# A two-layer MetaFormer kernel: 48 rows of image 0's convolution on VectorE, and the end of the third front dealt out among the first expert blocks

## The chip, the cores and the metric

The kernel runs on one NeuronCore of one Trainium2 chip. A time is the device time of one execution in microseconds (us). The kernel before took 3087.72 us, the median of three runs (3082.57 to 3088.3). The engines are named as in the profile: PE is TensorE (PEld its weight loads), DVE is VectorE, ACT is ScalarE, POOL is GpSimd, SP is SyncE, which here only issues transfers.

## The reference

Four images of 384 channels by 32x32 pixels (1024 tokens each) go through two layers:

```python
# layer 0
x = x + attention_with_relative_tables(ln_c(x))            # 8 heads
t = to_tokens(x); t = t + gelu(ln_t(t) @ kron(fc1, fc2).T) @ kron(proj1, proj2).T
# layer 1
x = x + dwconv7x7 + dwconv5x3 + dwconv3x5 + two separable pairs + bias   (of ln_c(x))
t = to_tokens(x); t = t + sum over 2 of 4 experts of gate * (gelu(ln_t(t) @ w1 + b1) @ w2 + b2)
x = from_tokens(t)
```

All depthwise kernels of layer 1 are folded into one 7x7 kernel per channel: 49 taps, each a multiply and an add over an image. The gate picks two of four experts for each token, so the rows of the expert stage are only known once an image has gone through its convolution.

## The kernel before, in words

Three stages follow each other. The projection to q, k, v and the attention take the first 1500 us and are not touched. `rest_phase` does everything after the attention, and the change lies in it.

For each image b the work of `rest_phase` is a row of generators; each `yield` is a step, and carries two costs, one for DVE and one for PE, in estimated us.

- `front(b)` (called by `enter`): loads, `project` (attention output projection, L977 and L980, then token statistics, L87 to L97) for two halves of 512 tokens, then `net` for each half. `net` is the small feed-forward net: `u_ps` (L999), DVE's `u` (L1001), twelve `f_ps` (L1012, a 32-row matmul), twelve Gelus on ACT (L1022), twelve `o_ps` (L1016), ACT's copy `o`, three `ffn_ps` (L1029) and three DVE additions into `xb` (L1030). The `f_ps` tiles rotate over the PSUM banks in `banks`: three banks of tag "h", and for image 0 three more from the pool `ps_y`.
- `normalise` (with front in `ahead`): per half the token statistics (`row_ps`, L87; `s_st`, L89; `s_rstd`, L96), two `all_ps` (L117, from `s_dg`, L115), and DVE's `xc` (L1061). `image` writes the padded image `img` (L1068).
- `convolve(b)`: for each of 49 taps DVE runs one multiply-add (L1089) for each of three chunks of 128 channels, over 32 rows. Its instructions keep the order in which they are issued. For image 0 (`first`) DVE only has chunk 0 and the first `own` rows of chunk 1; `taps_by_matmul` does the rest on PE with diagonal matrices (L1137, L1148) and adds it with L1151.
- `dispatch(b)`: `gates` (gate logits `gate_ps`, L661; statistics; softmax; top two), `scatter` (`before_ps`, L755; slot positions, ending with `pos`, L778; the list of expert blocks, `block_list`, ending with `slot`, L872; and 16 indirect transfers on POOL, L1205, that write the image's rows to `xs_d`).
- `blocks(g)`: the expert blocks of group g, 13, 16, 16 and 22 of them, 67 in all. A block is 128 rows: a gather `xg` by POOL (L1250), three transposes `xT_ps` (L1263), twelve times three `e_ps` (L1301), a Gelu (L1304) and a `y_ps` (L1279), then DVE's `yo` (L1282) and a store. POOL fetches weights `w` (L1269) into four tiles; a tile is free only after the `yo` of an earlier block. The first gather of group g waits for the rows that all dispatches up to image g have written (`g["after"]`).

What sets the order: each engine runs its instructions in one order. Image 0's `first` is dealt by hand with `ahead(1)`, then `dispatch(0)` with `ahead(2)`. Afterwards the loop in `more` deals the generator `todo` (`others()`: convolution 1, dispatch 1, convolution 2 together with front 3, dispatch 2, convolution 3, dispatch 3) among the expert blocks: after each `y` step it adds 0.05 to DVE's clock and 1.36 to PE's, and takes steps of `todo` as long as DVE's clock is behind PE's. When a group's blocks are all issued and the next group's rows are not, the rest of that dispatch is issued at once.

A position in the expert stage is counted below in blocks: 9.58 means that 9 blocks and 7 of 12 `y` steps of the tenth stand ahead on PE.

Of the kernel before, what the change touches and what calls it, by code (L numbers as in the profile page):

```python
# [19 lines left out]
B, C, IMG = 4, 384, 32  # L20
# [80 lines left out]
def result(steps):  # L101

    while True:
        try:
            next(steps)
        except StopIteration as end:
            return end.value


def to_partitions(nc, pools, ident, one, values):  # L110

    small, psum, tag = pools
    nj = values.shape[1]
    dg = small.tile([P, nj, P], F32, tag="s_dg", name="s_dg", bufs=1)
    nc.vector.tensor_tensor(dg, bcast(ident.unsqueeze(1), 1, nj), bcast(values, 2, P), ALU.mult)  # L115
    ps = psum.tile([P, TOK], F32, tag=tag, name="all_ps")
    nc.tensor.matmul(ps, one, dg.rearrange("p j n -> p (j n)"), start=True, stop=True)  # L117
    return ps


def center(nc, psum, tag, one, w):

    n = w.shape[2]
    for c in range(0, n, C):
        part = w[:, :, c : min(c + C, n)]
        ps = psum.tile([P, part.shape[2]], F32, tag=tag, name="sum_ps")
        for k in range(KC):
            nc.tensor.matmul(ps, one, part[:, k, :], start=(k == 0), stop=(k == KC - 1))
        for k in range(KC):
            nc.vector.scalar_tensor_tensor(part[:, k, :], ps, -1.0 / C, part[:, k, :], ALU.mult, ALU.add)  # L130
# [763 lines left out]
def rest_phase(tc, cst, x, ao_d, ins, xs_d, y_d, x2_d, out):  # L894
# [9 lines left out]
    with ExitStack() as es:  # L904
# [7 lines left out]
        ps_h = es.enter_context(tc.tile_pool(name="r_ps_h", bufs=3, space=PSUM))  # L912
        ps_y = es.enter_context(tc.tile_pool(name="r_ps_y", bufs=1, space=PSUM))
# [73 lines left out]

        def net(b, xs, rstd):

            banks = [(ps_h, "h", None)] * 3 + ([(ps_y, "y", 2)] * 2 + [(ps_y, "t", None)] if b == 0 else [])  # L990
            if True:
                scale = to_partitions(nc, (small, ps_m, "m"), ident, one, rstd)
                scale_sb = work.tile([P, TOK], F32, tag="scale", name="scale")
                nc.scalar.copy(scale_sb, scale)


                ps = ps_m.tile([P, TOK], F32, tag="m", name="u_ps")
                for k in range(KC):
                    nc.tensor.matmul(ps, fold[:, k, :], xs[:, k, :], start=(k == 0), stop=(k == KC - 1))  # L999
                u = small.tile([P, TOK], F32, tag="u", name="u")  # L1000
                nc.vector.tensor_tensor(u, ps, scale_sb, ALU.mult)  # L1001
                yield 1.4, 3.5

                po = ps_m.tile([P, TOK], F32, tag="m", name="o32_ps")
                pend = []
                for f0 in range(0, NF + 3, 3):
                    phs = []
                    for f in range(f0, min(f0 + 3, NF)):
                        pool, tag, bufs = banks[f % len(banks)]
                        ph = pool.tile([P, TOK], F32, tag=tag, name="f_ps", **({"bufs": bufs} if bufs else {}))  # L1010
                        lo = f % 4 * 32
                        nc.tensor.matmul(ph, c1t[lo : lo + 32, f // 4, :], u[lo : lo + 32, :], start=True, stop=True)  # L1012
                        phs.append((f, ph))
                    for f, hs in pend:
                        lo = f % 4 * 32
                        nc.tensor.matmul(  # L1016
                            po[lo : lo + 32, :], cp1t[:, f, :], hs, start=(f < 4), stop=(f >= NF - 4)
                        )
                    pend = []
                    for f, ph in phs:  # L1020
                        hs = hid.tile([P, TOK], F32, tag="hs", name="hs", bufs=HS)
                        nc.scalar.activation(hs, ph, AF.Gelu)  # L1022
                        pend.append((f, hs))
                    yield 0.0, 2.2
                o32 = small.tile([P, TOK], F32, tag="u", name="o32")
                nc.scalar.copy(o32, po)
                for m in range(KC):
                    ps = ps_h.tile([P, TOK], F32, tag="h", name="ffn_ps")
                    nc.tensor.matmul(ps, spread[:, m * P : (m + 1) * P], o32, start=True, stop=True)  # L1029
                    nc.vector.scalar_tensor_tensor(  # L1030
                        xs[:, m, :], ps, cp2[:, m : m + 1], xs[:, m, :], ALU.mult, ALU.add
                    )
                yield 2.1, 2.7
# [31 lines left out]
        def image(halves):  # L1065
            rows = IMG // 2
            for half, (xc, scale_sb) in enumerate(halves):
                nc.vector.tensor_tensor(  # L1068
                    img[:, :, 3 + half * rows : 3 + (half + 1) * rows, 3 : 3 + IMG],
                    xc.rearrange("p k (y x) -> p k y x", x=IMG),  # L1070
                    bcast(scale_sb.rearrange("p (y x) -> p y x", x=IMG).unsqueeze(1), 1, KC),
                    ALU.mult,
                )
                yield 1.7, 0.0
# [30 lines left out]
        def preload(w, keep=lambda ins_: ins_, which=range(2)):  # L1105
            for fh in which:
                keep(nc.sync.dma_start(w[fh], ins["w12"][fh * P : (fh + 1) * P, :]))
# [272 lines left out]
        def dispatch(b, pause=0.0):  # L1380
            yield from gates(b)
            yield from scatter(b, pause)

        def ahead(b, halves):
            if b < B:
                yield from enter(b)
                yield from normalise(xbs[b], halves)

        def first(halves, later):


            half, own = IMG // 2, 20
            taps = taps_by_matmul(xbs[0], made, [(2, 0, half), (2, half, half), (1, own, IMG - own)])
            yield from image(halves)
            for i, _ in enumerate(convolve(0, xbs[0], [(0, 0, IMG), (1, 0, own)])):
                for _ in range(1 + i % 4 // 2 + (i % 5 == 0)):
                    next(taps, None)
                if i % 7 < 5:
                    next(later, None)
                if i == 48:  # L1400
                    for steps in (taps, later):
                        for _ in steps:
                            pass
                yield
            preload(wts[1])

        def others():

            later = iter(())
            for b in range(1, B):
                if b > 2:
                    yield from image(halves[b])
                side, later = later, ahead(b + 1, halves[b + 1]) if b > 1 else iter(())
                for t, cost in enumerate(convolve(b, xbs[b], [(k, 0, IMG) for k in range(KC)])):
                    for start, steps in ((2, side), (12, later)):
                        more = next(steps, None) if t >= start else None
                        if more:  # L1420
                            cost = cost[0] + more[0], cost[1] + more[1]
                    yield cost
                yield from side
                yield from later
                later = dispatch(b, 0.0 if b == 2 else 2.6)
                if b == 1:
                    yield next(later)
                    yield from image(halves[2])
                    yield from later
            yield 6.0, 0.0  # L1430
            yield from later
# [9 lines left out]
        rstd0 = result(project(xs0, at0))  # L1441
        rstd1 = result(project(xs1, at1))
        result(net(0, xs0, rstd0))
        side = normalise(xbs[0], halves[0], (0,))
        for _ in net(0, xs1, rstd1):
            next(side, None)
# [3 lines left out]
        for _ in combined:  # L1450
            pass
        center(nc, ps_m, "m", one, gw)
        todo = others()
        made = diagonals((2, 1))
        for _ in first(halves[0], ahead(1, halves[1])):
            pass
        later = ahead(2, halves[2])
        for i, _ in enumerate(dispatch(0)):
            if i == 0:
                result(image(halves[1]))  # L1460
            for j in range(3 if i > 5 else 0):
                next(later, None)
                if i > 10 and (i + j) % 2:
                    next(todo)
        result(later)
        clock = [0.0, -8.0]

        def spend(steps):
            cost = next(steps, None)
# [125 lines left out]
```

## Time and profile before

| what | us |
|---|---|
| median of three runs | 3087.72 |
| time of the profiled execution | 3092.57 |
| its span | 3090.6 |
| PE busy | 2929.9 (95%) |
| DVE busy | 1956.6 (63%) |
| image 0's convolution, about | 1590 to 1737 |
| dispatch 0 and front 2, about | 1737 to 1842 |
| expert blocks with convolutions 1 to 3 | 1842 to 2560 |
| expert blocks alone, results | 2560 to 3090 |

The spans are from the start of the profiled execution. Where a line of the trace gives several numbers, they are the start, the duration, the engine, the line of the kernel and the operation, then the count, and in brackets the idle time of the engine before it and what ended that.

### The profile page before, as it was taken

The page shows a single profiled execution, that of the slowest core. Times are in us where ns is not written, and L with a number is a line of the kernel's source. Part 1 is how long each engine was busy: PE and PEld are TensorE (multiplying, and loading weights), DVE is VectorE, ACT ScalarE, POOL GpSimd, SP SyncE. Part 2 cuts the span into 40 slices and gives each one's busy share as a digit, 9 for nine tenths or more (in the row PEclk, how much of TensorE's full clock was granted, in tenths as well). Part 3 has the DMA queues.
Part 4 walks back from the last instruction along what each step waited for, and adds up shares of the span by engine and source line. Part 5 has one row for each costly group of instructions (what it writes and reads, how often), then busy time and mean ns, then how long its engine had stood idle before and what let it go on. Part 6 is the DMA issues. An engine that isn't in the chain of part 4 may idle for free.

```text
span 3090.6 us, 63376 instructions
## 1 busy us (share of the span) xinstructions
PE 2929.9 (95%) x25391; PEld 2020.6 (65%) x25391; DVE 1956.6 (63%) x3575; ACT 1370.8 (44%) x2833; POOL 1170.7 (38%) x1132
## 2 busy tenths in 40 slices
PE   8997999999999999999899789999999989999996
PEld 4544676777677677776533347776577867777775
DVE  2226787878787877777568869999899640001101
ACT  1104666666767666666322232333342243233332
POOL 3223747473747473737400122252124231124412
PEclk9998999999999999999999879999999999999998
DMA  3796565656565656564500314734243065366742
GB/s 123 259 320 212 130 203 131 206 132 203 134 202 134 200 131 196 136 199 128 186 21 34 128 31 156 274 136 154 75 175 132 26 229 215 134 227 250 263 180 72
DMA packets 262791, 500.55 MB, mean 162 GB/s; under 512 B 134736, under 2 KB 186832, under 8 KB 254816
## 3 DMA queue, kind: packets, MB, share of 16 engines
q1 hardware_dynamic: 169168, 247.12, 26.0%
q0 software_dynamic: 43424, 227.84, 20.0%
q10 hardware_dynamic: 49904, 21.53, 3.6%
q8 instruction: 200, 3.28, 0.5%
q14 instruction: 95, 0.78, 0.1%
HBM read 543.58 MB, written 152.37 MB: 225 GB/s over the span
## 4 chain that ended last, share of the span: by engine, by line
PE 67%; DVE 13%; issue 11%; POOL 4%; DMA 3%; ACT 2%; another core or an unknown queue 0%; SPq 0%; POOLq 0%; DVEq 0%; ACTq 0%
PE e_ps L1301 12%; PE y_ps L1279 12%; DVE xb L1089 8%; PE t_ps L410 7%; PE av_ps L227 7%; PE sc_ps L227 7%; PE tabq_ps L227 5%; PE a_ps L420 3%; PE tv_ps L227 2%; PE proj_ps L977 2%; PE tabk_ps L227 1%; PE tap_ps L1137 1%; DVE extra L402 1%; PE f_ps L1012 1%; PE o_ps L1016 1%
## 5 line engine op out<-in xcount | busy, mean ns | idle before, releaser
L1301 PEld LDWEIGHTS e_ps<-xT,w 128*128 128x128 f32 x4824 | 656.5, 193 | 217.7 <-issue 14.6
L353 POOL TENSOR_TENSOR bias<-b,s 128x416 f32<-128x416 f32 (+24 forms) x656 | 659.2, 1042 | 178.1 <-DMA s<-sd 157.5
L1301 PE MATMUL e_ps<-xT,w 128*128 128x128 f32 x4824 | 670.6, 277 | 14.1 <-DVE xb L1030 5.0
L1279 PE MATMUL y_ps<-w,eh 128*128 128x384 f32 x1608 | 651.9, 490 | 17.2 <-ACT eh L1304 14.8
L1089 DVE SCALAR_TENSOR_TENSOR xb<-img,pack,xb 128x1024 f32<-128x1024 f32 (+1 forms) x539 | 634.7, 1241 | 0.0
L1304 ACT ACTIVATE eh<-e_ps,w 128x128 f32<-128x128 f32 x804 | 292.9, 367 | 725.3 <-PE e_ps L1301 669.5
L1269 POOL DMA_INDIRECT w<-in_w,row x134 | 171.4, 1279 | 749.7 <-PE y_ps L1279 301.4
L402 DVE TENSOR_REDUCE extra<-arow 128x32 f32<-128x32 f32 (+24 forms) x768 | 381.3, 555 | 9.4 <-ACT arow L391 5.7
L381 DVE CUSTOM_DVE_ANT_0 arow<-sc_ps,bias 128x1024 f32<-128x1024 f32 x256 | 312.5, 1221 | 107.1 <-issue 55.5
L410 PEld LDWEIGHTS t_ps<-ident,arow 128*128 128x128 f32 x2048 | 221.2, 142 | 175.9 <-ACT aT L411 100.6
L391 ACT ACTIVATE arow<-arow,nm 128x1024 f32<-128x1024 f32 x256 | 302.4, 1181 | 70.8 <-DVE nm L381 70.8
L411 ACT COPY aT<-t_ps 128x512 f32<-128x512 f32 x512 | 278.6, 603 | 95.3 <-PE t_ps L410 95.0
L410 PE MATMUL t_ps<-ident,arow 128*128 128x128 f32 x2048 | 283.2, 282 | 17.1 <-ACT arow L391 17.0
L1282 DVE TENSOR_TENSOR yo<-y_ps,w 128x384 f32<-128x384 f32 x67 | 37.0, 553 | 396.0 <-PE y_ps L1279 387.8
L227 PE MATMUL sc_ps<-kk,qs 48*32 48x512 f32 x4096 | 279.2, 608 | 7.7 <-DVE nm L381 6.7
L1279 PEld LDWEIGHTS y_ps<-w,eh 128*128 128x128 f32 x1608 | 248.3, 193 | 31.9 <-ACT eh L1304 19.4
L227 PEld LDWEIGHTS av_ps<-aT,vb 128*64 128x64 f32 x4096 | 222.3, 137 | 52.0 <-ACT aT L411 40.4
L227 PE MATMUL av_ps<-aT,vb 128*64 128x128 f32 x4096 | 237.7, 274 | 0.0
L318 DVE STREAM_TRANSPOSE b<-tabk_ps 128x480 f32<-128x480 f32 x256 | 218.4, 983 | 23.5 <-PE tabk_ps L227 22.2
L227 PE MATMUL tabk_ps<-tab,kq 48*128 48x480 f32 x512 | 223.0, 582 | 6.1 <-DVE b L318 6.1
L227 PE MATMUL tabq_ps<-tab,kq 48*128 48x480 f32 x512 | 220.1, 579 | 2.1 <-ACT aT L411 1.4
L322 ACT COPY st<-tabq_ps 128x480 f32<-128x480 f32 x256 | 142.3, 560 | 71.0 <-PE tabk_ps L227 45.0
(211 smaller groups left out, 3163.4 us busy)
## 6 DMA issues: line engine op xcount, KB each, us to landing
sd<-st SPq DMA_DIRECT2D x128, 480.0 KB
s<-sd SPq DMA_DIRECT2D x256, 240.0 KB
xs_d<-zero POOLq DMA_DIRECT2D x8, 3072.0 KB
tvw<-in_tv SPq DMA_DIRECT2D x120, 192.0 KB
y_d<-yo SPq DMA_DIRECT2D x67, 192.0 KB
qk_d<-qk_sb POOLq DMA_DIRECT2D x48, 256.0 KB
qs<-qk_d SPq DMA_DIRECT2D x256, 48.0 KB
kq<-qk_d ACTq DMA_DIRECT2D x56, 192.0 KB
```

The source lines that it names most:

```text
L227: ins = nc.tensor.matmul(*args, **kw)
L318: turn = nc.vector.transpose(b2.rearrange("p e y x -> p x (e y)")[:, i + j], ps[:, j, : SPAN * IMG])
L353: nc.gpsimd.tensor_tensor(bias[:, y0:y1, :], bass.AP(b2.tensor, b2.offset + (e * IMG + y0) * IMG, [list(b2.ap[0]), [(step * IMG + 1) * IMG ...
L381: nc.vector.tensor_tensor_reduce(s["flat"], ps.rearrange("p h n -> p (h n)"), s["bias"].rearrange("p y x -> p (y x)"), -SCALE, BIG, ALU.ad ...
L391: nc.scalar.activation(s["flat"], s["flat"], AF.Exp, bias=s["nm"], scale=-1.0, accum_out=dn[:, y % YT : y % YT + 1])
L402: pin(nc.vector.tensor_reduce(ex[:, i, :], a[:, p0:p1, :].rearrange("p y x -> p x y"), AX.X, ALU.add))
L410: pin(nc.tensor.transpose(pt[:, j, :], s["flat"][:, k0 : k0 + P], ident))
L411: pin(nc.scalar.copy(aT[:, 4 * g : 4 * g + 4, s["y"] % YB, :], pt))
L1089: ins_ = nc.vector.scalar_tensor_tensor(acc[:, k, y0:y1], img[:, k, dy + y0 : dy + y1, dx : dx + IMG], w7[:, k, dy, dx : dx + 1], acc[:, k ...
L1279: nc.tensor.matmul(py, hs, w[:, o : o + C], start=(ff == 0), stop=(ff == NF - 1))
L1301: nc.tensor.matmul(ph, w[:, o : o + P], xT[k][:, c, :], start=(c == 0), stop=(c == KC - 1))
L1304: nc.scalar.activation(hs, ph, AF.Gelu, bias=w[:, o : o + 1])
```

## The change

Four edits. Image 0: DVE takes 16 rows of chunk 1 instead of 20 (48 rows with chunk 0), PE the other 16, and the taps are dealt at a slightly different pace. `net` of image 2 also uses the three banks of `ps_y`. During `dispatch(0)` two steps of front 2 are taken per step instead of three, and one step of convolution 1 instead of one or two alternately; what is left of front 2 is not finished on the spot, but goes step by step with `todo`. The clock of DVE's work starts at -15 instead of -8.

```diff
 def net(b, xs, rstd):
-    banks = [(ps_h, "h", None)] * 3 + ([(ps_y, "y", 2)] * 2 + [(ps_y, "t", None)] if b == 0 else [])
+    banks = [(ps_h, "h", None)] * 3 + ([(ps_y, "y", 2)] * 2 + [(ps_y, "t", None)] if b in (0, 2) else [])
...
 def first(halves, later):
-    half, own = IMG // 2, 20
+    half, own = IMG // 2, 16
...
-        for _ in range(1 + i % 4 // 2 + (i % 5 == 0)):
+        for _ in range(1 + i % 4 // 2 + (i % 4 == 0)):
             next(taps, None)
...
+def mixed(some, others_):
+
+    while True:
+        steps = [next(s, None) for s in (some, others_)]
+        if not any(steps):
+            return
+        yield tuple(sum(c) for c in zip(*filter(None, steps)))
...
 for i, _ in enumerate(dispatch(0)):
     if i == 0:
         result(image(halves[1]))
-    for j in range(3 if i > 5 else 0):
+    for _ in range(2 if i > 5 else 0):
         next(later, None)
-        if i > 10 and (i + j) % 2:
-            next(todo)
-result(later)
-clock = [0.0, -8.0]
+    if i > 10:
+        next(todo)
+todo = mixed(later, todo)
+clock = [0.0, -15.0]
```

## The prediction

> **What bounds the kernel now.** First the page's slices (40 of 77 us each). The change touches slices 21 to 31.
>
> ```profile
> PE   8997999999999999999899789999999989999996
> ...
> DVE  2226787878787877777568869999899640001101
> ...
> PEclk9998999999999999999999879999999999999998
> ```
>
> PE is above 90% nearly everywhere; the hole is the front stage (slices 22 to 24), where its clock drops too. DVE is as full as PE in the five slices after it. Next, windows over these stretches (busy time of each engine, granted clock, DMA):
>
> ```profile
> core 0: us, PE busy (x) PEld busy (x) DVE busy (x) ACT busy (x) POOL busy (x), PEclk, DMA share, GB/s
> 1780.00:1790.00 10.00, 10.00 (x30) 2.18 (x26) 0.14 (x3) 3.37 (x6) 7.09 (x8) 0.59 0.33 111
> ...
> 1820.00:1830.00 10.00, 5.89 (x29) 3.46 (x28) 9.60 (x23) 0.30 (x1) 1.00 (x1) 0.79 0.08 25
> ...
> 1840.00:1990.00 150.00, 149.40 (x912) 118.37 (x911) 149.80 (x170) 44.47 (x120) 37.76 (x24) 1.00 0.46 174
> 1990.00:2058.00 68.00, 65.20 (x393) 49.13 (x392) 61.44 (x156) 31.37 (x69) 38.03 (x27) 1.00 0.65 247
> 2058.00:2390.00 332.00, 323.42 (x1848) 231.87 (x1846) 321.04 (x484) 118.99 (x274) 82.94 (x62) 0.99 0.34 126
> ```
>
> From 1840 to 2390 both engines are full: no slack on either. Third, the timeline of PE: image 0's net (six banks, first two lines) and image 2's (three banks).
>
> ```profile
> 1543.69 1.99 PE L1012 MATMUL f_ps<-u,pack 32*128 32x512 f32 x12 [1.08 <-DVE u L1001]
> 1545.61 1.92 PE L1016 MATMUL o_ps<-hs,pack 128*32 128x512 f32 x6
> ...
> 1773.46 2.97 PE L1012 MATMUL f_ps<-u,pack 32*128 32x512 f32 x6 [1.19 <-ACT hs L1022]
> 1776.36 1.93 PE L1016 MATMUL o_ps<-hs,pack 128*32 128x512 f32 x6
> ```
>
> A float32 matmul is two instructions here, so the x12 are six f and the x6 three. Image 2's take twice as long after the wait of 1.19 us for a bank. DVE meanwhile stands 12.44 us before L1030. Last, and decisive, the start of a group: image 1's gate on PE and group 1's first transposes; POOL's first and last row writes, weights and gather; then the chain at group 2's start.
>
> ```profile
> 1993.36 2.77 PE L661 MATMUL gate_ps<-xb,pack 128*32 128x512 f32 x12
> ...
> 2057.79 0.49 PE L1263 MATMUL xT_ps<-ident,xg 128*128 128x128 f32 x3
> ```
> ```profile
> 2018.45 1.01 POOL L1205 DMA_INDIRECT xs_d<-rows,pos  x1 [5.29 <-DVE b_prod L860]
> ...
> 2048.25 0.96 POOL L1205 DMA_INDIRECT xs_d<-rows,pos  x1 [0.30 <-issue]
> 2049.51 2.10 POOL L1269 DMA_INDIRECT w<-in_w,row  x1 [0.30 <-issue]
> 2051.92 2.07 POOL L1250 DMA_INDIRECT xg<-xs_d,slot  x1 [0.31 <-issue]
> ```
> ```profile
> 2386.52 2.48 DVE xb L1089 x2
> ...
> 2389.03 3.48 DMA xg<-xs_d,slot
> ...
> 2392.64 0.89 PE xT_ps L1263 x3
> ...
> 2394.08 4.21 PE e_ps L1301 x18
> ```
>
> Group 1's rows land just as PE gets there; at group 2 PE already waits some 4 us for the gather. From gate to next group there is a latency that PE has to cover with blocks of the old group, and it has nothing to spare.
>
> **What the Trainium skill says.** "TensorE: Matmul & The Clock Gate", Part 1, has PE at half clock after an idle window of about 3.4 us: the trace agrees in the factor (1.14 us for six f instructions at 1771, 2.97 at 1773). The same page, under "Architectural detail", calls VectorE a strict FIFO: agrees, ready L1089 instructions stand behind L1030 for 12.44 us. "SBUF — State Buffer", "Who interferes with whom", has GpSimd blocked by VectorE instructions with two SBUF inputs: compatible with row writes of 0.97 or 2.0 us while L1089 runs. "ScalarE: Activation LUTs", "What ACT_TABLE_LOAD costs", gives about 1283 ns; the trace has 1283.
>
> **Part by part.** Positions are read from the built kernels' order on each engine.
>
> *48 rows.* A DVE step of 1024 and 640 elements takes 2.01 us (ten instructions in 10.04), three of 1024 take 3.6: so 0.81 for 640, 1.0 ns an element, 49 x 0.13 = 6.4 us less. PE's 196 tap instructions grow from 64x384 to 64x512: 0.082 to 0.112 us apiece (20 less 8 instructions: 1.35 us; 48 less 8 at 384: 3.3), 5.9 us more. From 1620 to 1690 PE is the fuller one (DVE idles 14 us), and the last tap sum now has two steps behind it, not one. I take 0, between -4 (DVE alone decides) and +3.
>
> *Six banks for image 2.* No instruction more. A half at full clock takes 9.7 us (1543.7 to 1553.4), against 18.3 (1771.1 to 1789.4). If the clock still drops, the first six f at 1.99 and the rest at half rate (six f at 2.87 / 3, twelve o at 1.93 / 3): 15.5. DVE now has one step of convolution 1 (3.7 us) ahead of `u`, so f starts about 3 us later, at 1774.4, after more PE idle time than in image 0's case (3 us against 1.1). So half clock is likely in at least one half; I take one of two.
>
> *The rest of front 2 in the blocks.* The first e_ps comes at 1774.4 + 15.5 + 9.6 (half to half, as before: 1789.4 to 1799.0) + 9.7 + 1.3 (xT) = 1810.5, against 1830. The moved part (one ffn, 12 + 12 transposes, four all_ps, four table loads) costs PE in the blocks what front 3 costs there: the two yo intervals around it (2211.9, 2235.6, 2254.8) are 10.7 us above two blocks of 16.1, and 2.6 for ffn. It issues no transfer; on SP image 1's store and image 3's loads fall behind eleven stores of y instead of nine, but front 3 reads them only at 16.9, some 90 us on. Counted as if all blocks ran evenly from it, the start is 1810.5 + 13.3 = 1823.8; before it is 1993.4 - 9.58 x 16.1 = 1839.1. Gain 15.3 (9.5 both halves at half clock, 21 none).
>
> *Convolution 1 and dispatch 1 come later in the order.* Four steps fewer before the blocks, the clock at -15, and front 2's costs put image 1's gate at position 11.25 instead of 9.58, behind yo 10 instead of yo 8. DVE needs 14.9 us for its twelve taps and yo, PE 16.1 a block, so DVE waits at every yo and cannot be early: the gate runs at 1823.8 + 11.25 x 16.1 = 2004.9, 11.5 later than before. From gate to the first block then: 25.1 to the first write (1993.36 to 2018.45), 26 for sixteen writes (27.5 before without the two weight fetches, 24.6 at group 2), 7.8 from the last write's end to e_ps (2386.3 to 2394.1): 58.9 us. PE has 1.75 blocks and 9.3 us of gate work for it: 37.5. It waits 21 us for the gather, where it waited for nothing, and starts cold (half clock for 6.8 us, 3.4 lost). All sixteen writes now stand on POOL behind group 0's last fetch and ahead of group 1's first, so that fetch waits too, but it is no later than the gather. Group 1 starts 11.5 + 58.9 + 3.4 - 64.4 = 9.5 us later than before.
>
> *Group 2.* Image 2's gate moves from 22.75 to 23.5, its before_ps from 26.33 to 27.08: `rank` (L759) follows yo 26 by one tap instead of yo 25 by four, 16.1 - 3.8 = 12 us later against group 1's start. The 46 us from L759 to group 2 (2347.8 to 2394.1) are the same. Shift 9.5 + 12 = 21.5. A second count on DVE alone: between the two slot lists both kernels have 231 taps, but yo 13 now makes DVE idle about 14 us: 22. After group 2 nothing waits (image 3's gate is at 35.17 in both, group 3 at 45) and the shift reaches the end.
>
> **Sum.** On the profiled execution: 3090.6 + 0 + 21.5 = 3112 span, 2 more for its time. The median of the runs is 4.9 below the profiled time: 3087.7 + 21 = 3109.
>
> **Rivals.** *Faster:* the saved front is kept, because gate to first block takes less than PE's cover. It decides below 37.5 us at the first gate; the rows' writes would have to go in about 5 us. Then 15 to 21 us are gained: 3070. For it: PE's hole is real. Against: sixteen writes never took less than 21.7 us (image 0's). *Only the first gate waits:* DVE catches up in the wait and image 2's dispatch is not late: +9.5, 3097. Against: DVE's order ties it to yo 26. *Cancels:* full clock in both halves and 22 us of writes at the first gate, no second wait: 3087. *DVE loses more,* both halves at half clock and DVE's waits at front 3 on top: +33, 3121.
>
> **Chances.** Both waits, 3098 to 3117: 0.68. First gate only: 0.12. Worse: 0.07. Cancels: 0.04. Faster: 0.09. Change that this measurement can't tell from none is 0.2%, 6 us. Slower 0.86, the same 0.05, faster 0.09. The range 3088 to 3123 leaves out the faster case and little above.
>
> **What would show it.** f_ps of image 2 in runs of twelve instructions; first e_ps near 1810; gate of image 1 near 2005; POOL's sixteen writes unbroken, ending near 2056; PE idle about 20 us before group 1's first xT_ps and 10 to 15 before group 2's, DMA xg as releaser. No such idle time at group 1, or a gate before 1990, makes me wrong.

## The result and the profile after

The changed kernel took 3119.3 us (median of 3106.17, 3119.91, 3125.24 and 3118.7), the kernel before 3087.94 on the same chip (four runs each): 1.0101 times as long, with an interval of 1.0077 to 1.0124. That is 31 us slower, where 21 were forecast. In profiled executions the difference is smaller, 3106.17 against 3092.57 us (spans 3104.2 and 3090.6): the profiled execution after is the fastest of its four, and the one before is longer than its median. So the changed kernel was profiled a second time, on another chip (e4_again, 3116.3 us of span), and this execution is near its median. Below, these two are the first and the second profile after.

The slices of the page of the kernel after, the same rows as before:

```profile
PE   8997999999999999999899899979998999999996
...
DVE  2226787878787878787477879879999740001101
...
PEclk9998999999999999999999899989999999999998
```

The hole in the front (slices 23 and 24: 78 before) is nearly filled, 89, and the clock with it (87 before, 89 after). Two new holes stand further on: a 7 in slice 27, with an 8 of clock, and an 8 in slice 31. Windows over the same stretches of the kernel after, with one more for the second hole:

```profile
1780.00:1790.00 10.00, 10.00 (x35) 3.44 (x32) 7.53 (x15) 3.34 (x6) 7.40 (x7) 1.00 0.29 98
1820.00:1830.00 10.00, 9.86 (x52) 6.63 (x51) 7.97 (x14) 1.58 (x4) 0.88 (x1) 1.00 0.05 20
1840.00:1990.00 150.00, 149.49 (x914) 118.47 (x914) 140.99 (x167) 47.55 (x122) 39.02 (x26) 1.00 0.60 226
1990.00:2058.00 68.00, 47.47 (x268) 34.75 (x267) 55.51 (x149) 25.16 (x52) 24.98 (x18) 0.86 0.36 126
...
2390.00:2420.00 30.00, 10.72 (x53) 8.30 (x52) 29.45 (x34) 2.77 (x8) 23.54 (x15) 0.66 0.26 86
```

From 1820 to 1830 PE is busy for 9.86 us instead of 5.89. Between 1990 and 2058 it is busy for 47.5 instead of 65.2, and from 2390 on for 10.7 of 30. And DVE, which had no slack from 1840 to 1990 (149.8 of 150), now idles 9 us there: its convolution steps were dealt out later. From the first e_ps to image 1's gate it idles 28 us (before 2.9), most of it in one wait before L1030.

What opened the holes is in the timelines of the kernel after. PE: image 1's gate and the first transposes of group 1. POOL: first and last row write, weights, gather. Then the chain of work (the steps that ended last) at group 2's start.

```profile
2000.09 2.77 PE L661 MATMUL gate_ps<-xb,pack 128*32 128x512 f32 x12
...
2061.62 0.90 PE L1263 MATMUL xT_ps<-ident,xg 128*128 128x128 f32 x3 [20.08 <-DMA xg<-xs_d,slot]
```
```profile
2029.11 1.03 POOL L1205 DMA_INDIRECT xs_d<-rows,pos  x1 [30.23 <-DVE b_change L853]
...
2053.80 2.02 POOL L1205 DMA_INDIRECT xs_d<-rows,pos  x1 [0.31 <-issue]
2056.13 1.04 POOL L1269 DMA_INDIRECT w<-in_w,row  x1 [0.30 <-issue]
2058.23 1.25 POOL L1250 DMA_INDIRECT xg<-xs_d,slot  x1 [1.06 <-DMA xs_d<-rows,pos]
```
```profile
2404.87 3.69 DVE xb L1089 x3
...
2408.57 4.19 DMA xg<-xs_d,slot
...
2412.90 0.89 PE xT_ps L1263 x3
...
2414.34 3.81 PE e_ps L1301 x18
```

The 16 writes are unbroken, and PE waits 20.08 us for the gather behind them; before, the first transposes of group 1 had no wait. At group 2 PE waits 18.7 us (before 4.0).

A table of five points is the ruler for everything below, because image 0's gate alone varies by 7 us between the profiles of this study. All are us from that gate (`gate_ps`, 1736.68 before, 1733.45 and 1737.74 after); in brackets PE's wait for xg.

| profile | first e_ps | image 1's gate | group 1's first xT_ps | group 2's first xT_ps | end of span |
|---|---|---|---|---|---|
| before | 93.7 | 256.7 | 321.1 (0) | 656.0 (4.0) | 1353.9 |
| after | 72.4 | 266.6 | 328.2 (20.1) | 679.5 (18.7) | 1370.8 |
| after, once more | 79.8 | 274.0 | 335.5 (22.4) | 685.8 (18.7) | 1378.6 |

The first e_ps comes 14 to 21 us earlier; at image 1's gate this has turned into a loss of 10 to 17, at group 2 of 24 to 30.

### The profile page after: what moved, and what is told of

It reads as the page before. It is cut to its first block, busy times and chain, and to the rows that moved or that the text cites. A ratio compares the mean times of both kernels' runs of the same rounds, so it can differ in the third digit from the quotient of the medians.

```text
span 3104.2 us, 63372 instructions
## 1 busy us (share of the span) xinstructions
PE 2921.3 (94%) x25391; PEld 2014.4 (65%) x25391; DVE 1950.2 (63%) x3575; ACT 1375.0 (44%) x2835; POOL 1179.6 (38%) x1132
## 4 chain that ended last, share of the span: by engine, by line
PE 74%; DVE 9%; issue 8%; DMA 4%; POOL 3%; ACT 2%; SPq 0%; another core or an unknown queue 0%; POOLq 0%; ACTq 0%; DVEq 0%
PE e_ps L1301 16%; PE y_ps L1279 15%; PE t_ps L410 7%; PE sc_ps L227 7%; PE av_ps L227 7%; PE tabq_ps L227 5%; DVE xb L1089 4%; PE a_ps L420 3%; PE tv_ps L227 2%; PE tap_ps L1137 1%; PE proj_ps L977 1%; POOL bias L353 1%; PE tabk_ps L227 1%; DMA s<-sd 1%; PE f_ps L1012 1%
## 5 line engine op out<-in xcount | busy, mean ns | idle before, releaser
L1301 PE MATMUL e_ps<-xT,w 128*128 128x128 f32 x4824 | 671.3, 277 | 13.6 <-ACT xT L1264 6.5
L1089 DVE SCALAR_TENSOR_TENSOR xb<-img,pack,xb 128x1024 f32<-128x1024 f32 (+1 forms) x539 | 628.4, 1229 | 0.0
L1279 PEld LDWEIGHTS y_ps<-w,eh 128*128 128x128 f32 x1608 | 247.5, 193 | 28.3 <-ACT eh L1304 15.4
L1205 POOL DMA_INDIRECT xs_d<-rows,pos x64 | 80.7, 1260 | 295.8 <-DVE b_prod L860 231.3
```

Source lines behind the costliest of these rows:

```text
L1089: ins_ = nc.vector.scalar_tensor_tensor(acc[:, k, y0:y1], img[:, k, dy + y0 : dy + y1, dx : dx + IMG], w7[:, k, dy, dx : dx + 1], acc[:, k ...
L1279: nc.tensor.matmul(py, hs, w[:, o : o + C], start=(ff == 0), stop=(ff == NF - 1))
L1301: nc.tensor.matmul(ph, w[:, o : o + P], xT[k][:, c, :], start=(c == 0), stop=(c == KC - 1))
```

## The experiments

The runs were made in three sets of four, each set on another chip, with the kernel before beside them (3082.8, 3080.2 and 3068.6 us): so the ratios are compared, and times from different sets are not. Ratios are to the kernel before on the same chip, with their intervals; where a ratio is put in us, it is its difference from 1 (or from another ratio) times 3085 us. Of e2_rows, e5_early, e8_half, e10_early_nobanks and e11_earlier the profiled execution is 4 to 9 us faster than the median of the runs, so their points belong to a fast execution, as those of the first profile after do.

**e1_banks: only the banks.** The kernel before with

```diff
-    ... if b == 0 else [])
+    ... if b in (0, 2) else [])
```

> The kernel before with one edit: image 2's net uses six PSUM banks. My account: the order of the instructions is the same as before on every engine (image 1's gate at position 9.58), so nothing else becomes late; the two halves of the net shorten from 18.3 us each to between 9.7 and 15.5, the first e_ps moves from 1830 to between 1812 and 1820, DVE's wait before L1030 (21.4 us) shrinks by as much, and the whole expert stage moves with it: 10 to 18 us faster, about 3074, with xT_ps of group 1 at about 2043 and no wait there. Rival, DVE is the bound of this stretch and the banks only move the wait: within 5 us of the kernel before. Rival, PE's half clock in the net has nothing to do with the banks: the halves stay at 18 us, no change.

Measured: 0.9975 (0.9966 to 0.9984), 8 us faster; first e_ps at 89.0, image 1's gate at 252.4, group 1 at 316.5, group 2 at 650.6. The sign is as expected, the size below the range of 10 to 18 us. Timeline of PE in this run, the two halves of image 2's net:

```profile
1764.97 1.99 PE L1012 MATMUL f_ps<-u,pack 32*128 32x512 f32 x12 [0.85 <-DVE u L1001]
...
1790.72 2.97 PE L1012 MATMUL f_ps<-u,pack 32*128 32x512 f32 x12 [2.58 <-DVE u L1001]
1793.62 1.99 PE L1016 MATMUL o_ps<-hs,pack 128*32 128x512 f32 x6
1795.54 2.08 PE L1012 MATMUL f_ps<-u,pack 32*128 32x512 f32 x6
```

The first half starts at full clock (twelve instructions in 1.99) and takes 14.4 us, 2.4 of them idle; the second, after an idle time of 2.58, falls to half clock and takes 14.9. Before it was 18.2 and 17.8. All that is gained at the first e_ps (4.7 us) is still there at group 2 (5.4): with the order of the work unchanged, a saved front is kept.

**e2_rows: only the rows.** The kernel before with

```diff
-            half, own = IMG // 2, 20
+            half, own = IMG // 2, 16
...
-                for _ in range(1 + i % 4 // 2 + (i % 5 == 0)):
+                for _ in range(1 + i % 4 // 2 + (i % 4 == 0)):
```

> The kernel before with one edit: VectorE has 16 rows of chunk 1 of image 0 instead of 20 and the pace of the taps goes with it. The prediction took 0 (between -4 and +3); the profile of the changed kernel had image 0's gate at 1733.45 instead of 1736.68, so 3 us faster: 3085. Rival: PE is the bound and the gate is not earlier: 3088 to 3091.

Measured: 1.0003 (0.9993 to 1.0012), no difference; the prediction's 0 was right, and the 3 us that I read out of the first profile after were not the edit's. The rival has the mechanism. On this chip image 0's gate stood at 1730.27 with 16 rows and at 1730.19 with 20 (e1_banks). Only the wait before it is shorter (4.14 us against 7.54): PE, with more taps, is later, and DVE still ends the wait. DVE's saving went into longer waits for PE: from 1590 to 1731 us it stands 13.7 us before L1030 (9.7 with 20 rows) and 4.0 before `u` (2.2).

**e3_deal: only the dealing.** The changed kernel with 20 rows, the old pace and three banks for image 2, so `mixed`, the steps of `dispatch(0)` and the clock at -15 are what is left of the change.

> The changed kernel without its other two edits: 20 rows and three banks in image 2's net as before, but front 2 and convolution 1 dealt as in the changed kernel. My account: the dealing is the whole loss and more, image 1's gate stays at position 11.25 and PE waits about 20 us at group 1 and about 19 at group 2, while the banks' gain is missing: 15 to 20 us slower than the changed kernel, about 3136. Rival, the banks are worth nothing here: the same as the changed kernel, 3119. Rival, the loss comes from the banks or the rows: 3088.

Measured: 1.0175 (1.0158 to 1.0192), 54 us slower than the kernel before; the changed kernel in the same set 1.0103. So the dealing, with its clock at -15, is the whole loss, and the other edits take 22 us of it back, where 15 to 20 were expected. That is more than e1_banks, for a reason that the timeline of PE shows:

```profile
1778.12 1.13 PE L1012 MATMUL f_ps<-u,pack 32*128 32x512 f32 x6 [0.85 <-DVE u L1001]
1794.16 0.90 PE L1263 MATMUL xT_ps<-ident,xg 128*128 128x128 f32 x3 [14.91 <-DMA xg<-xs_d,slot]
1794.99 2.08 PE L1012 MATMUL f_ps<-u,pack 32*128 32x512 f32 x6
```

Here the first transposes of group 0 stand in PE's order between two groups of f, where their rows are not yet there, and the whole net waits 14.91 us behind them. In the changed kernel they stand behind both halves. The edits are not independent: banks and rows also decide where this instruction falls.

**e4_again: the changed kernel once more.**

> The changed kernel once more. Its first four times were 3106.2 to 3125.2 us, and the mean granted clock of the three long ones was 0.972 against 0.976: 0.004 of 3110 us is 12 us of full clock, or 25 us more at half clock. My account: the net of image 2 runs at full clock in some executions and at half in others; a profile near 3120 shows x12 f_ps of 3 us and more in both halves and a first e_ps near 1815 to 1820. Rival: the two waits of PE vary (writes of rows, 25 to 30 us): then e_ps is at 1806 again and the waits at groups 1 and 2 are 5 to 10 us longer together.

Measured: 1.0103 (1.0086 to 1.012), and a profile of 3116.3 us. Timeline of PE, first half of image 2's net, in the first profile after (upper) and in this one (lower):

```profile
1770.83 3.40 PE L1012 MATMUL f_ps<-u,pack 32*128 32x512 f32 x12 [0.57 <-DVE u L1001]
...
1775.97 1.12 PE L1012 MATMUL f_ps<-u,pack 32*128 32x512 f32 x2
...
1780.05 1.13 PE L1012 MATMUL f_ps<-u,pack 32*128 32x512 f32 x6
```
```profile
1774.86 4.37 PE L1012 MATMUL f_ps<-u,pack 32*128 32x512 f32 x12 [0.57 <-DVE u L1001]
...
1781.01 2.07 PE L1012 MATMUL f_ps<-u,pack 32*128 32x512 f32 x2
...
1788.73 2.08 PE L1012 MATMUL f_ps<-u,pack 32*128 32x512 f32 x6
```

The same instructions, with the same waits before them (2.05 and 0.57 us): in one execution the clock is back some 5 us after the first f, in the other only for the last 2 of the half's 19.3 us. The two halves take 13.0 and 12.1 us there, 19.3 and 13.5 here. That is 7.7 us more; the first e_ps is 7.4 later from image 0's gate, and the end 7.8 (1378.6 and 1370.8). The rival, longer waits, has 2.3 us at group 1 and nothing at group 2. The rest of the 12 us between the spans had passed before image 0's gate, which is 4.3 us later here.

**e5_early: the same kernel, gates earlier.** The changed kernel with

```diff
-        clock = [0.0, -15.0]
+        clock = [0.0, 8.0]
```

> The changed kernel with one number: DVE's clock starts at 8 instead of -15. More of convolution 1 is issued before the blocks, and image 1's gate stands at position 9.75 again (11.25), image 2's before_ps at 26.5 (27.08), nearly as in the kernel before. My account (the positions make the waits): from gate to group 1's first xT_ps about 62 us passed in every run so far; DVE had 10.5 us of idle time left between 1830 and 1990, so the gate can come about 10 us earlier, the wait at group 1 goes, and from group 1 to group 2 it is 335 us again instead of 351: 24 us less than the changed kernel, about 3094. Rival, the new dealing of front 2 loses the time, wherever the gate stands: 3112 to 3120. Rival, DVE falls behind and PE waits for yo: also above 3110, with PE idle before y_ps in the first blocks.

Measured: 0.9993 (0.9984 to 1.0002); the ratio of the changed kernel is 1.0101, so one number is worth 33 us. Nothing of front 2, the banks or the rows is touched. Timeline of PE in this run:

```profile
1980.67 2.77 PE L661 MATMUL gate_ps<-xb,pack 128*32 128x512 f32 x12
...
2043.57 0.52 PE L1263 MATMUL xT_ps<-ident,xg 128*128 128x128 f32 x3 [1.18 <-DMA xg<-xs_d,slot]
```

From gate to group it is 62.9 us, much as in the changed kernel (61.5); but the gate is 22 us earlier, at 244.6, and the wait is 1.18. Group 2 starts at 645.8 after a wait of 7.5. The direction was expected and the size was not (24): I had counted DVE's idle time from 1830 on only. DVE also stood 20.7 us before L1030 in the changed kernel, and with more convolution steps ahead of it 6.6 here. In this profile group 2 starts 10 us earlier than before (645.8 and 656.0), but by the ratio the runs gain only 2.

**e6_late: the kernel before, gates later.**

```diff
-        clock = [0.0, -8.0]
+        clock = [0.0, -25.0]
```

> The kernel before with one number: DVE's clock starts at -25 instead of -8. Nothing of front 2 and no bank is changed, only image 1's gate goes to position 10.67 (9.58) and image 2's before_ps to 27.0 (26.33). My account: the gate comes about 17 us later (1.09 blocks of 16.1), group 1's first xT_ps waits some 12 us for the gather and is about 15 us later, group 2's waits 12 to 16: 25 to 30 us slower than the kernel before, about 3111. Rival, the loss of the changed kernel comes from front 2's rest between the blocks and not from the order of the gates: within 6 us of the kernel before.

Measured: 1.009 (1.0073 to 1.0107), 28 us slower. This is what was expected. First e_ps at 95.1, near its place before (93.7); image 1's gate at 274.4, group 1 at 330.9 after a wait of 9.7, group 2 at 678.8 after 15.1. Timeline of PE in this run, image 1's gate and the first transposes of groups 1 and 2:

```profile
2005.43 2.77 PE L661 MATMUL gate_ps<-xb,pack 128*32 128x512 f32 x12
...
2061.85 0.87 PE L1263 MATMUL xT_ps<-ident,xg 128*128 128x128 f32 x3 [9.66 <-DMA xg<-xs_d,slot]
...
2409.75 0.87 PE L1263 MATMUL xT_ps<-ident,xg 128*128 128x128 f32 x3 [15.05 <-DMA xg<-xs_d,slot]
```

So a loss nearly as large as the changed kernel's comes without any of its other edits, by the place of the gates alone.

**e7_both: banks, rows and the gates a little earlier.** The kernel before with both edits and `clock = [0.0, 0.0]`.

> The kernel before with the six banks for image 2, the 16 rows, and DVE's clock at 0 instead of -8: image 1's gate at position 9.08, image 2's before_ps at 25.83. My account: the banks' 7.7 us stay, DVE is full before image 1's gate, so group 1 is not earlier, but image 2's dispatch is 8 us ahead and the wait of 4 us at group 2 and the half clock after it go: 3070 to 3073. Rival, DVE's extra six instructions ahead of the first yo make PE wait for yo: 3077 or more.

Measured: 0.9995 (0.9985 to 1.0005), no gain, against the expectation. Image 1's gate is at 241.2 and image 2's `before_ps` 12 us earlier than before, but PE still waits 4.04 us at group 2. POOL's timeline of this run:

```profile
2350.33 1.94 POOL L1205 DMA_INDIRECT xs_d<-rows,pos  x1 [0.30 <-issue]
2354.59 1.95 POOL L1269 DMA_INDIRECT w<-in_w,row  x1 [2.32 <-DVE pause L1097]
2356.84 2.01 POOL L1205 DMA_INDIRECT xs_d<-rows,pos  x1 [0.31 <-issue]
...
2380.03 0.97 POOL L1205 DMA_INDIRECT xs_d<-rows,pos  x1 [0.30 <-issue]
```

A fetch of weights stands between the second and the third write and waits for a tile, and eight of the sixteen writes take the long time of about 2 us (before: four): 32.9 us from the first write to the end of the last (2348.06 to 2381.00), 24.6 before. An earlier `pos` only helps if POOL's queue lets it. The rival has its part too: up to 2050 PE waits 2.3 us for `yo` and 4.7 for weights, whose tile a `yo` has to free.

**e8_half and e9_half1: half of the writes.** The changed kernel without half of the row writes, so that half of the rows are missing in the expert stage, for images 1 and 2 (e8_half) or image 1 alone (e9_half1; there the condition is `b == 1`),

```diff
-                for s in range(2):
+                for s in range(0 if b in (1, 2) and j > 3 else 2):
                     write(rows, im["pos"][:, j, s : s + 1])
```

> The changed kernel with half of the 16 row writes of images 1 and 2 left out, so that half of these images' rows are missing in the expert stage. Positions of gates as in the changed kernel. My account: the writes are a link of the chain from the gate to the next group; eight of them take 13 us less (1.63 us each), so PE's waits for xg shrink from 20 and 19 us to about 7 and 6, if the gates themselves keep their times, and the kernel takes about 26 us less than the changed one: 3092. Rival, the block list on DVE or the weights' fetch ends the wait, not the writes: waits as before, 3117.

> The changed kernel with half of the 16 row writes of image 1 alone left out (half of that image's rows are missing in the expert stage); image 2 writes all. Positions as in the changed kernel. The question is whether the first wait counts, or only the second. My account: both waits add up; group 1 starts about 13 us earlier, image 2's gate with it, the wait at group 2 stays at 19 us: about 15 us less than the changed kernel, 3102. Rival, the wait at group 1 is given back at group 2: group 2 starts when it did and its wait grows to 30 us: 3117.

Measured: e8_half 1.0004 (0.9992 to 1.0015), e9_half1 1.0065 (1.005 to 1.0079). In us below the changed kernel: 30 and 11. PE in e8_half, starts of groups 1 and 2:

```profile
2046.13 0.90 PE L1263 MATMUL xT_ps<-ident,xg 128*128 128x128 f32 x3 [8.02 <-DMA xg<-xs_d,slot]
...
2383.46 0.52 PE L1263 MATMUL xT_ps<-ident,xg 128*128 128x128 f32 x3 [0.88 <-DMA xg<-xs_d,slot]
```

From gate to group 1 it is 47.3 us in e8_half and 47.2 in e9_half1 instead of 61.5: eight writes are 14 us, and the writes, not the block list, are the last link. In e9_half1 group 1 comes at 317.4, its wait is 8.0; group 2's wait is 16.3 and the way between them 353.7 (351.3): the waits add up, and about 2 of the 14 us are given back.

**e10_early_nobanks: what the banks are worth once the gates are in time.** e5_early with three banks for image 2.

> The kernel e5_early (changed kernel with DVE's clock at 8) with three banks for image 2's net. Image 1's gate stands at position 9.75, before_ps of image 2 at 26.5. My account: with the gates in time, the banks are worth what they were worth in the kernel before, 8 us (the two halves of the net 18 us each instead of 12 to 17): about 3086. Rival, the banks are worth 20 us in the new dealing, as the difference of e3_deal and the changed kernel: about 3098.

Measured: 1.0027 (1.0016 to 1.0038); e5_early has 0.9993, so the banks are worth 10 us. Group 1 stands at 317.4 and group 2 at 657.9, 10 and 12 later than in e5_early. The 8 us of the first account are nearer than the rival's 20.

**e11_earlier and e12_fill: a faster version.** e11_earlier is the changed kernel with `clock = [0.0, 16.0]`. e12_fill is the kernel before with six banks, the rows, and

```diff
-                if i > 10 and (i + j) % 2:
+                if i > 10 and (i + j) % 3:
                     next(todo)
...
-        clock = [0.0, -8.0]
+        clock = [0.0, -15.0]
```

> The changed kernel with DVE's clock at 16: image 1's gate at 9.25, image 2's before_ps at 26.0. My account: DVE is full before image 1's gate, so group 1 is not earlier than in e5_early, but the 7.5 us wait at group 2 shrinks to 0 to 4: 3070 to 3075, the fastest of this study. Rival, six more taps ahead of the first yo hold PE up in the first blocks: 3080 or more.

> The kernel before with the six banks, the 16 rows, and during dispatch 0 convolution 1's steps taken at two of three steps of front 2 instead of one of two, with DVE's clock at -15 to make up for it (image 1's gate at position 9.0, image 2's before_ps at 25.75). My account: one more step of convolution stands ahead of the second half's L1030, where DVE waited 6 us, so DVE gains up to 3.7 us and PE nothing: 3070 to 3077. Rival, the additional steps delay the first yo and PE waits for it: 3080 or more.

Measured: e11_earlier 0.9977 (0.997 to 0.9985), e12_fill 0.9973 (0.9965 to 0.9981), 7 and 8 us faster than the kernel before, both in the ranges expected if these are counted from e5_early and the kernel before beside it; with e1_banks (0.9975) these are the three fastest, and their intervals don't tell them apart. All three beat both kernels. In e11_earlier group 2's wait fell from 7.5 us to 1.3; the expectation had 0 to 4. In e12_fill DVE stands 3.4 us before L1030, and both halves of the net run at full clock (10.2 and 9.7 us).

## Why the prediction was right, and what was mis-sized

The time, 3119.3, lies in the range (3088 to 3123); the forecast was 10 us too low. It is 2 us above the stretch from 3098 to 3117 that was given 0.68, so by the time alone it falls under "worse", given 0.07; the mechanism is the one that was forecast, two waits for xg behind later gates. By its own steps, positions counted from image 0's gate where that helps:

*48 rows, 0:* right (e2_rows).

*Six banks, one half of the net at half clock and the other at full, 25.2 us in all:* the sum is what the first profile has (13.0 and 12.1), but the form is wrong. Neither half is all at one clock, and the execution near the median needs 32.8 (19.3 and 13.5). This is the largest mis-sized term, 7.6 us. Half clock is not all of it. In the changed kernel the first half's f and o alternate once more (f in runs of 12, 2, 4 and 6 instructions instead of 12, 6 and 6), and a run of two takes as long as one of six (1.12 and 1.13 us in the first profile, 2.07 and 2.08 in the second). In e8_half this half takes 12.7 us at a granted clock of 1.00; in e7_both and e12_fill, with the old order and six banks, 10.2. The price of half clock was not the clock's alone either: the lines at 1771 and 1773, 1.14 and 2.97 us, are a factor of 2.6 apart. At half clock six f instructions take 2.87 us with three banks and 2.08 with six, at full clock 1.13. The first e_ps, forecast at 73.8 from the gate, came at 72.4 and 79.8.

*The rest of front 2 in the blocks, 13.3 us:* from first e_ps to image 1's gate there are 194.2 us in both profiles after; less 11.25 blocks of 16.1 that is 13.1. In the kernel before the same way has 8.8 us above its 9.58 blocks, so counted in even blocks the front saves 16.9 us in the first profile and 9.6 in the second, where 15.3 was forecast.

*The gate at position 11.25, and PE's wait of 21 us at group 1:* right (20.1 and 22.4), but its parts were not. The chain from gate to e_ps, 58.9, took 63.0 in both profiles: 29.0 to the first write (26.7 in the second profile) instead of 25.1, 26.7 (28.0) for the writes instead of 26, and 7.3 (8.3) after them. The first link grew because `before_ps` has its place on PE behind blocks: DVE had the mask ready and waited 5.85 us (3.5 in the second profile, before 1.7) for it. In the first profile PE ran at half clock there (0.50 from 2014.9 to 2021.5) after waits of 2.29 and 1.39 us for a Gelu; in the second, after 2.29 and 1.64, at full clock. What made this link longer was PE's own work and its own waits, so the wait for xg did not grow with it.

*Group 1 9.5 us later, group 2 another 12, in all 21.5:* from before to after 7.1 and 14.4 us at group 1, 23.5 and 29.8 at group 2. Of the 9.5, the 3.4 for a cold start belong behind the first xT_ps and so to the next stretch: that one grew by 16.4 and 15.4, where 12 + 3.4 had been counted. Here too parts made up for each other: PE was at half clock for 4.4 and 5.7 us after group 1's first xT_ps, not 6.8, so the cold start cost 2 to 3 us; and the way from image 2's `before_ps` to group 2, taken as the same, grew from 46.0 to 48.6, because the sixteen writes took 27.0 us instead of 24.6. The wait at group 2, named as 10 to 15 us, was 18.7. A slip in the sum is 1.1 us: 58.9 ends at the first e_ps, the 64.4 set against it at the first xT_ps. The second profile, which stands for the median, is 8 us above the forecast, and 6 of these are what it lost against the first one in the net. That the first profile comes within 2 us of the forecast is partly luck: it is the fastest of four.

*After group 2 nothing waits and the shift reaches the end:* the order was right, the word nothing was not. From group 2's start to the end the profile before has 697.9 us, those after 691.3 and 692.8; e2_rows, whose work from there on is in the order of the kernel before, has 688.5 on another chip. In the profile before some 1.7 us more were lost in dispatch 3 (around 2525 to 2560) and 4.4 in the result rows between 2780 and 2960. So about 6 us of the small profiled difference (13.6) are the profile before, not the change; whether chip or execution, these runs don't settle; the chip has a part, since this stretch takes 687 to 693 us in all eight profiles of the first two sets and 675 to 677 in all four of the third. The medians, 31 apart, are close to the 29.8 at group 2.

*The rivals.* Faster would have needed gate to first block in 37.5 us; it took 63. Only the first gate: refuted by the trace (18.7 at group 2) and by e9_half1. Cancels: the writes took 26.7 us and more, never 22. DVE loses more (+33, 3121): the time is nearer to this rival than to the forecast, and its first part, half clock in both halves, is nearly what the second profile shows (32.8 us, where two times 15.5 had been counted). Its second part, DVE's waits at front 3 on top, has no room: from group 1 to group 2 about as much was lost (16.4 and 15.4) as had been counted without it (15.4).

The front's saving was real, and it was spent in waits. The gate had been moved behind 1.67 more blocks, and what PE did sooner it then did ahead of the gate instead of behind it, where the rows' 60 us or so need cover. e5_early and e6_late show it from both sides: the gate's place without the change costs 28 us, the change with the gate nearly in its place (9.75; before 9.58) costs nothing.

## What to carry to other kernels

When a producer's result needs a fixed time to come back (here 56 to 63 us from gate to rows, where PE waited for them), count how much independent work stands behind the producer in the consumer's order, not how early the consumer starts: work moved ahead of the producer is cover taken away. Where work is dealt by a clock, its start value is part of any change of a stage: one number decided here between 1.0% slower and 0.2% faster. And an edit's worth holds for one order only: the banks were worth 8 us in one, 10 in another, and 22 (with the rows) where they also moved an instruction out of the net.

## What the hardware did that was not expected

In the second profile after, PE stayed at half clock for 17 us of the net's first half (granted clock 0.50 from 1775.2 to 1792.2) with no idle time between its f and o matmuls; in the first, with the same waits of 2.05 and 0.57 us ahead of it, for 3.4 us (0.50 from 1772.5 to 1775.8). Ahead of the second half an idle time of 2.46 us brought half clock in the first profile, and the half took 12.1 us; in e9_half1, with the same order and the same wait, PE stayed at full clock, and the half took 9.7. The Trainium skill, "TensorE: Matmul & The Clock Gate", Part 1, has PE at half clock after an idle window of about 3.4 us and back after one busy window of the same length, with windows that run freely. The scatter from run to run fits windows that run freely; that single waits of less than 3.4 us were enough, and 17 us at half rate, don't fit an idle window of 3.4 us and a return after 3.4 busy us. What kept the clock down, the small matmuls (32 rows in or 32 columns out) or something else, was not tried.

The long row writes on POOL go with DVE's convolution. Of the 872 writes (L1205) in the 14 profiles, 359 had no L1089 of DVE beside them, and none of these took more than 1.46 us; all 191 that took more than 1.5 us had one beside them for at least 46% of their time. But many writes beside an L1089 were short as well, and no run changed this alone, so it is a count and not a proof.
